# adaLN block on one core: a preparation with every engine in source order, statistics before conditioning, and one group's operands moved first

## The chip, the core and the metric

The kernel runs on one core of a Trainium2 chip. The core has five engines with instruction queues of their own: TensorE (PE, matmuls and transposes, with a weight load that the profile shows as PEld), VectorE (DVE), ScalarE (ACT), GpSimd (POOL) and SyncE (SP). [...] The metric is the device time of one execution in microseconds (us), the median of three runs.

## The reference, cut to what matters

Four sequences (B = 4) of 1024 rows with 256 features go through an attention and a feed-forward layer. A condition vector per sequence gives shift, scale and gate for both.

```python
mod = (_silu(L0_c) @ L0_wmod).reshape(L0_c.shape[0], 6, 1, -1)
sa, ca, ga, sb, cb, gb = (mod[:, 0], mod[:, 1], mod[:, 2], mod[:, 3], mod[:, 4], mod[:, 5])
...
h = _layernorm(x, axis=-1) * (1 + ca) + sa
x = x + ga * _L0_attn_ref(h, L0_attn_xpos, L0_attn_qkv_w, L0_attn_proj_w, L0_attn_proj_b)
h = _layernorm(x, axis=-1) * (1 + cb) + sb
x = x + gb * _L0_ffn_ref(h, L0_ffn_W_base, L0_ffn_b_base, L0_ffn_W_enc, L0_ffn_b_enc, L0_ffn_W_dec, L0_ffn_b_dec, L0_ffn_W_down, L0_ffn_b_down, L0_ffn_W_up, L0_ffn_b_up, L0_ffn_connected_idx)
```

The attention has 16 heads of 16 features and a softmax. The feed-forward layer finds, for each sequence of 256 rows in the reference's view, which of eight small encoders and decoders restores its input best, and adds that one's adapter to a common linear layer. `ga` and `gb` are kept at least 0.25 from zero.

## The kernel before, in words

**The work and its tiles.** A batch is taken as eight tiles of 128 rows, in two halves of 512 (half 0 and half 1). The heads are in four groups of four; a (batch, group) pair is the unit of the attention. For each there is a pass that finds the row maxima of the scores (`ps`, line 448, reduced by DVE into `mx`, line 455), a short way that turns those maxima into a row and stores it as matmul operand (`pmx` L416, `mfull`, POOL's `mrow`, a write to DRAM by L423 and a read-back `mt` by L431), and a pass that computes the scores again with the maximum subtracted by a second matmul (`pt`, L542), takes their exponential on ACT (`es`, L550) and multiplies by v (`pv`, L506). The second pass of a group runs beside the first pass of the next. Queries and keys are each split into two parts of shorter mantissa (`qhl`, `khl`, L348 and L349), and `expand` (L393 to 403) moves them by DMA into the operand tiles `q64`, `k64`: for one group and one pair of heads four transfers of 128 KB for q and four for k, so 16 for a group.

**The preparation**, before the loop over the groups. `load_two` (L84) brings two tiles of x at a time; `qn` is the qkv weight as it lies in memory, `wm` the modulation weight, `pn` the projection's. Then, in source order:

- `condition` (L140 to 151): two transposes of the condition (`pc`), an exponential on ACT, and three small DVE operations that end in `cs`, the sigmoid-weighted condition.
- `turn_weights` (L153): two transposes of one 128-row part of a weight (`pw`) and a copy by ACT. Parts 0 to 3 are q and k, 4 and 5 are v.
- `modulation` (L160): 16 matmuls with `cs` (`pm`, L167) and two DVE copies into `modc`, the shift and scale.
- `norm_first`, a list of work items from `norm_items` (L252): for each half four times `bn_stats` and `bn_aggr` (L260, L261), `ve` (L265), POOL's `rstd` (L267), four centrings (`xh`, L272, on DVE for batch 0 and on POOL for the others), transposes `ptn` (L284) and ACT's `hT` with shift and scale (L285), which needs `modc`.
- `qk_chunk` (L326): the projection of q and k for groups 0 and 1, `expand` for groups 0 and 1, constants, memsets (L921, L937, L942) and `load_rest` (L199 to 215).
- The first sixteen maxima of group 0, with the items of `beside` among them, one after each: the turns of weights 4 and 5, four tiles of v (`pvp`, L370), the second modulation, the gates' rows (`pg`, L182, which POOL shapes and SP writes to DRAM), the turns of the projection weight and the biases.

**What sets the order.** PE's order is the order in the source (`manual_schedule`). In the preparation and in the rest, the order of DVE, ACT, POOL and SP is found by the framework's scheduler, which places instructions by modelled costs; an instruction of a later part can thus go ahead of an earlier one. Each engine works in its order and waits where its next instruction has to wait. In the built program a DMA issue waits until the transfer eight issues earlier has landed.

**The steady stage** (from the loop over `order`, 256 steps, 64 for a batch) is planned in the source: streams of items, of which "X" runs at once, "D" and "R" take a place on PE, "wait" holds a stream for so many steps, "need" until another item is done, "at" and "by" give a step. `defer(n, f)` calls f after n ticks (one tick a step). `turned` (L463) and its `flip`, `back` and `scaled` carry the sums of the softmax through DRAM and multiply by their reciprocal; `post` (L556) is the projection, second norm and feed-forward layer of the batch before; `fixed` (L997) loads, norms and projects the next batch.

Of the kernel before, what the change touches and what calls it, by code (L numbers as in the profile page):

```python
# [17 lines left out]
P = 128  # L18
# [8 lines left out]
def tile_adaln_block(  # L27
# [21 lines left out]
    nc = tc.nc  # L49
    B, S, D = x.shape  # L50
    NE, _, FH = w_enc.shape
    R = w_down.shape[2]
    NT = S // P
    NC = D // P
# [6 lines left out]
    TH = HALF // P  # L61
# [17 lines left out]

    prep = ExitStack()  # L80
    stage = prep.enter_context(tc.tile_pool(name="stage", bufs=1))
    ctx.enter_context(tc.manual_schedule(engines={mybir.EngineType.PE}))

    def load_two(b, u):  # L84
        src = x[b].rearrange("(t p) d -> p t d", p=P)
# [10 lines left out]
    qn = stage.tile([P, 3 * NC, D], F32, name="qn")  # L96
# [1 line left out]
    nc.scalar.dma_start(qn[:, : 2 * NC, :], qkv_rows[:, : 2 * NC, :])  # L98
    wm = stage.tile([P, NC, 6 * D], F32, name="wm")
    wmod_rows = wmod.rearrange("(c p) e -> p c e", p=P)  # L100
    nc.sync.dma_start(wm[:, :, : 2 * D], wmod_rows[:, :, : 2 * D])
    for u in range(NT // 4, NT // 2):
        x_in[0, u] = load_two(0, u)
    nc.scalar.dma_start(qn[:, 2 * NC :, :], qkv_rows[:, 2 * NC :, :])
    nc.scalar.dma_start(wm[:, :, 2 * D :], wmod_rows[:, :, 2 * D :])
    pn = stage.tile([P, NC, D], F32, name="pn")
    nc.scalar.dma_start(pn, proj_w.rearrange("(o p) i -> p o i", p=P))


    ident = cst.tile([P, P], F32, name="ident")  # L110
# [42 lines left out]
    def turn_weights(dst, src, o, tile):  # L153

        pt = tile([P, NC, P], f"pw_{dst.name}_{o}")
        for c in range(NC):
            nc.tensor.transpose(pt[:, c, :], src[:, o, c * P : (c + 1) * P], ident)
        nc.scalar.copy(dst[:, :, o * P : (o + 1) * P], pt)
# [74 lines left out]
    def defer(steps, f):  # L233
        later.append([steps, f])
# [228 lines left out]
    def turned(b, ch, h):  # L463

        n = ch * NH + h
        few = [GC * HG * HALF // P, P]
        rs = st.tile([P, few[0]], F32, tag="rs", name=f"rs_{b}_{ch}_{h}", bufs=2)
        nc.sync.dma_start(rs, sdram[n].rearrange("j (a c) -> (j a) c", c=few[0]))

        def flip():  # L470
            nc.vector.reciprocal(rs, rs)
            nc.sync.dma_start(rdram[n].rearrange("j (a c) -> (j a) c", c=few[0]), rs)

        def back():
            su = wp.tile([P, HALF], F32, tag="su", name=f"su_{b}_{ch}_{h}", bufs=1)
            nc.sync.dma_start(su, rdram[n].unsqueeze(1).to_broadcast([GC * HG, HD, HALF]))
            defer(1, lambda: scaled(b, ch, h, su))

        defer(1, flip)
        defer(2, back)  # L480

    def scaled(b, ch, h, su):
        part = aT_of[b, h][:, ch, :]
        nc.gpsimd.tensor_tensor(part, part, su, ALU.mult)  # L484
# [10 lines left out]
    def step_of(b, g):  # L495

        n = b * NG + g
        va = vaug[n % NV]
        ch, r0 = g // GC, (g % GC) * HG * HD
        acc = {}  # L500

        def weigh(h, kt, es):
            if kt == 0:
                acc[h] = accp.tile([P, HALF], F32, tag="acc", name=f"pv_{b}_{g}_{h}")
            for j in range(HG):
                nc.tensor.matmul(  # L506
                    acc[h][j * STRIP : (j + 1) * STRIP, :],
                    va[:, kt, j, :],
                    es[j // 2][:, j % 2, :],
                    start=(kt == 0),  # L510
                    stop=(kt == NT - 1),
                )
            if kt == NT - 1:
                if (b, h) not in aT_of:
                    aT_of[b, h] = wp.tile([P, NC, HALF], F32, tag="aT", name=f"aT_{b}_{h}", bufs=3)
                ou = wp.tile([P, HALF], F32, tag="ou", name=f"ou_{b}_{g}_{h}", bufs=1)
                nc.scalar.copy(ou, acc[h])
                to = slice(r0, r0 + HG * HD)
                nc.sync.dma_start(aT_of[b, h][to, ch, :], ou[0::2, :])
                if (b, ch) == (B - 1, NC - 1):  # L520
                    if h not in last_su:
                        last_su[h] = wp.tile([P, HALF], F32, tag="su", name=f"su_{b}_{ch}_{h}", bufs=1)
                    nc.sync.dma_start(last_su[h][to, :], ou[1::2, :])
                    if g == NG - 1 and h < NH - 1:
                        defer(2, lambda: scaled_last(h))
                        defer(4, lambda: done.add((b, ch, h)))
                    return
                j0 = (g % GC) * HG
                nc.sync.dma_start(sdram[ch * NH + h][j0 : j0 + HG, :], ou[1::STRIP, :])
                if g % GC == GC - 1:  # L530
                    defer(1, lambda: turned(b, ch, h))
                    defer(8, lambda: done.add((b, ch, h)))

        def begin(h, kt, i, es):

            pt = big_tile([P, 2, HALF], f"pt_{b}_{g}_{h}_{kt}_{i}")
            hs = slice(h * HALF, (h + 1) * HALF)
            q, k = duos["q", b, g, i], duos["k", b, g, i]
            for first in (True, False):
                for a in range(2):  # L540
                    r = slice(a * DUO, (a + 1) * DUO)
                    nc.tensor.matmul(  # L542
                        pt[:, a, :],
                        k[r, kt * P : (kt + 1) * P] if first else picks[i][r, :],
                        q[r, hs] if first else mt[n % 2][r, hs],
                        start=first,
                        stop=not first,
                    )
            e = wp.tile([P, 2, HALF], F32, tag="es", name=f"es_{b}_{g}_{h}_{kt}_{i}", bufs=4)
            nc.scalar.activation(e, pt, AF.Exp, scale=SCALE)  # L550
            es.append(e)

        return begin, weigh


    def post(b, last=False):  # L556
# [231 lines left out]
        def rec(pr, h):  # L788
            return [("R", lambda c=c: decode(pr, c, h)) for c in range(NC)]

        main = [("need", (b - 1, "end")), ("X", load), ("X", alloc), ("wait", 1), ("X", gate_proj)]
        main += [("X", lambda u=u: biased(u, "gpb")) for u in range(NT // 2)]
        for h in range(NH):
            main += [("need", (b, ch, h)) for ch in range(NC)]
# [7 lines left out]
                encs += [("take", "half"), enc(pr, h), ("done", (b, pr, "e", h))]  # L802
                recs += [("need", (b, pr, "e", h))] + rec(pr, h) + [("give", "half")]
        recs.append(("done", (b, "r")))
        tail = [("need", (b, "r")), ("wait", 3), ("D", 0.1, [choose]), ("X", gate_out)]
        tail += [("X", lambda u=u: biased(u, "gbb")) for u in range(NT // 2)]
        tail += [("wait", 1), ("D", FULL, [lambda c=c: narrow(c) for c in range(NC)]), ("wait", 1)]
        each = [(u, t) for u in range(NT // 2) for t in range(2)]
# [69 lines left out]
    def all_of(*streams, most=10**9):  # L878

        took = True  # L880
        while took and most > 0:
            took = False
            for s in streams:
# [5 lines left out]
                if item is not None:  # L889
# [3 lines left out]
                    took, most = True, most - 1  # L893
                    break

    cs = condition()
    for o in range(2 * NC):
        turn_weights(wqkv, qn, o, big_tile)
    modulation(SA, big_tile)
    all_of(Stream(norm_first(0)))  # L900
    all_of(Stream(qk_chunk(0, 0)))
    for g in range(2):
        for i in range(2):
            expand(0, g, i)
    mean_w = cst.tile([P, P], F32, name="mean_w")
    nc.gpsimd.memset(mean_w, 1.0 / (S * D))
    iota_i = cst.tile([P, NE], I32, name="iota_i")
# [48 lines left out]
    nc.gpsimd.tensor_tensor(part_r, part_f, upper, ALU.add)  # L956


    beside = [lambda o=o: turn_weights(wqkv, qn, o, spare_tile) for o in range(2 * NC, 3 * NC)]
    beside += [lambda item=item: [f() for f in item[2]] for item in v_all(0)]  # L960
    beside += [lambda: modulation(SB, spare_tile), lambda: gate_rows(spare_tile)]
    beside += [lambda o=o: turn_weights(wproj, pn, o, spare_tile) for o in range(NC)]
    beside.append(lambda: turn_biases(spare_tile))
# [1 line left out]
    FIRST = PAIRS // NH  # L965
    for n in range(FIRST):
        next(maxima)
        if beside:
            beside.pop(0)()
    tick()  # L970
    all_of(Stream(list(urgent)))
# [2 lines left out]
    tick()  # L974
    given = FIRST + 4
    prep.close()
    wp = ctx.enter_context(tc.tile_pool(name="wp", bufs=2))

    def all_maxima():
# [17 lines left out]
    def fixed(b):  # L997

        moves, work = [], []
        k0 = b * BATCH  # L1000

        def moved(g, i):
            return ("X", lambda: expand(*groups[b * NG + g + 2], i))

        for g in range(NG):
            if b + 1 < B or g < NG - 2:
                key = ("qk", b + (g + 2) // NG, (g + 2) % NG // GC)
                moves += [("at", k0 + g * STEPS + 1), ("need", key), moved(g, 0), moved(g, 1)]
                moves.append(("done", ("moved", b, g)))
        if b + 1 < B:  # L1010

            def load(u):
                x_in[b + 1, u] = load_two(b + 1, u)

            between = [("need", (b - 1, "n", 0))] if b else []
            first = norm_first(b + 1, between + [("X", lambda: load(NT // 2 - 1))])
            if b == 0:
                work += qk_chunk(0, 1) + [("by", 8), ("done", ("qk", 0, 1))]
            work += [("X", lambda u=u: load(u)) for u in range(NT // 2 - 1)] + [("wait", 2)] + first
            work += [("need", ("moved", b, 1)), ("wait", 2)] + qk_chunk(b + 1, 0)  # L1020
            work += [("by", k0 + 2 * STEPS + 8), ("done", ("qk", b + 1, 0))]
            work += [("at", k0 + 3 * STEPS + 1)] + v_all(b + 1)
            work += [("need", ("moved", b, 3)), ("at", k0 + 3 * STEPS + 5)] + qk_chunk(b + 1, 1)
            work += [("by", k0 + 4 * STEPS), ("done", ("qk", b + 1, 1))]
        return [moves, work]
# [180 lines left out]
```

## Time and profile before

| what | value |
|---|---|
| median of three runs | 1190.61 us (1190.61, 1190.59, 1194.73) |
| profiled execution | 1194.91 us |
| its span | 1193.1 us |
| mean granted PE clock | 0.978 of full |
| PE, DVE, ACT, POOL busy | 90%, 66%, 58%, 21% of the span |
| matmuls | 6324 |

The profile comes from one profiled execution, whose time is 4.30 us above the median of the runs; the span is the time from its first to its last record. A page gives the busy time of each engine, then the span in 40 equal slices, in which a digit is the busy share in tenths. Groups of instructions follow with their line, tile names (out<-in), count, busy time and mean. Other views are taken from the same trace: a table of stretches, the timeline of one engine (start, duration, operation, count, and in brackets the idle time before it with what ended it), waits, and the chain of waits, which goes back from the last instruction through what released each step. "issue" is time in which an engine waited for nothing that the profile shows.

### The profile page before, as it was taken

The page shows a single profiled execution, that of the slowest core. Times are in us where ns is not written, and L with a number is a line of the kernel's source. Part 1 is how long each engine was busy: PE and PEld are TensorE (multiplying, and loading weights), DVE is VectorE, ACT ScalarE, POOL GpSimd, SP SyncE. Part 2 cuts the span into 40 slices and gives each one's busy share as a digit, 9 for nine tenths or more (in the row PEclk, how much of TensorE's full clock was granted, in tenths as well). Part 3 has the DMA queues.
Part 4 walks back from the last instruction along what each step waited for, and adds up shares of the span by engine and source line. Part 5 has one row for each costly group of instructions (what it writes and reads, how often), then busy time and mean ns, then how long its engine had stood idle before and what let it go on. Part 6 is the DMA issues. An engine that isn't in the chain of part 4 may idle for free.

```text
span 1193.1 us, 16436 instructions
## 1 busy us (share of the span) xinstructions
PE 1077.8 (90%) x6324; PEld 476.5 (40%) x6324; DVE 791.9 (66%) x975; ACT 692.3 (58%) x928; POOL 254.8 (21%) x271
## 2 busy tenths in 40 slices
PE   4768889999999889999999889999999889899995
PEld 3423333434444333345444333345444333344443
DVE  4477977777687666767678666676778777701264
ACT  2114466665666677654556667654655676647662
POOL 3155000200314002240224201140222200042003
PEclk9869999999999999999999999999999999999998
DMA  6522130122121201113131200204040300011001
GB/s 203 142 81 55 41 77 18 50 69 54 44 60 36 61 15 48 54 43 82 38 110 27 56 15 24 64 27 103 17 131 8 76 1 18 15 58 53 18 1 47
DMA packets 42582, 63.92 MB, mean 54 GB/s; under 512 B 13052, under 2 KB 28436, under 8 KB 42504
## 3 DMA queue, kind: packets, MB, share of 16 engines
q1 hardware_dynamic: 40000, 58.41, 18.2%
q10 hardware_dynamic: 1736, 3.15, 0.8%
q0 software_dynamic: 768, 1.31, 0.5%
q8 instruction: 50, 0.82, 0.3%
q14 instruction: 28, 0.23, 0.1%
HBM read 19.39 MB, written 5.19 MB: 21 GB/s over the span
## 4 chain that ended last, share of the span: by engine, by line
PE 69%; ACT 11%; DVE 10%; DMA 4%; issue 4%; POOL 2%; SPq 0%; ACTq 0%; DVEq 0%; POOLq 0%
PE pt L542 18%; PE pv L506 18%; PE ps L448 10%; ACT es L550 6%; DVE mx L455 5%; PE ph L626 4%; PE pr L647 3%; PE pq L338 3%; PE pvp L370 3%; ACT df L655 3%; DVE df L650 3%; PE ppj L591 2%; PE pf L761 2%; PE pk L338 2%; PE ptn_n L284 2%
## 5 line engine op out<-in xcount | busy, mean ns | idle before, releaser
L455 DVE TENSOR_REDUCE mx<-ps 128x2 f32<-128x1024 f32 x512 | 611.8, 1220 | 191.9 <-PE ps L448 188.2
L550 ACT ACTIVATE es<-pt 128x1024 f32<-128x1024 f32 x512 | 510.8, 1022 | 296.2 <-PE pt L542 289.5
L506 PE MATMUL pv<-es,vaug 128*32 128x512 f32 x2048 | 274.6, 607 | 0.1
L448 PE MATMUL ps<-k,q 64*128 64x512 f32 x1024 | 236.4, 461 | 35.0 <-ACT es L550 10.4
L542 PE MATMUL pt<-q,k 64*128 64x512 f32 x1024 | 239.0, 451 | 21.8 <-ACT es L550 10.7
L542 PE MATMUL pt<-mt,pick 64*128 64x512 f32 x1024 | 209.4, 393 | 4.6 <-DMA mt<-mdram 4.6
L448 PEld LDWEIGHTS ps<-k,q 64*128 64x128 f32 x1024 | 98.3, 186 | 201.4 <-issue 92.5
L542 PEld LDWEIGHTS pt<-q,k 64*128 64x128 f32 x1024 | 99.3, 184 | 170.7 <-DVE mx L455 96.8
L655 ACT ACTIVATE df<-df,fbias 128x512 f32<-128x512 f32 x128 | 91.1, 713 | 55.0 <-DVE df L650 55.0
L542 PEld LDWEIGHTS pt<-mt,pick 64*128 64x128 f32 x1024 | 100.4, 186 | 15.6 <-DMA mt<-mdram 5.8
L650 DVE TENSOR_TENSOR df<-pr,h2T 128x1024 f32<-128x1024 f32 x64 | 77.4, 1222 | 42.5 <-PE pr L647 20.7
L506 PEld LDWEIGHTS pv<-es,vaug 128*32 128x32 f32 x2048 | 40.5, 108 | 100.1 <-issue 90.8
L647 PE MATMUL pr<-he,wdec 64*128 64x512 f32 x256 | 64.3, 614 | 6.3 <-ACT es L550 6.2
L484 POOL TENSOR_TENSOR aT<-aT,su 128x512 f32<-128x512 f32 x14 | 17.8, 1273 | 238.9 <-DMA su<-rdram 189.5
L626 PE MATMUL ph<-h2T,wenc 128*128 128x512 f32 x128 | 63.6, 623 | 0.0
L781 DVE TENSOR_TENSOR x<-pf,x 128x512 f32<-128x512 f32 x16 | 10.8, 687 | 54.3 <-PE pf L772 22.1
L353 POOL CAST qhl<-fu_q 128x512 fp32r<-128x512 f32 x14 | 8.5, 610 | 178.4 <-ACT fu_q L352 175.9
L267 POOL TENSOR_TENSOR rstd_n<-ve_n,neghalf 128x4 f32<-128x4 f32 x16 | 16.8, 1048 | 102.2 <-DVE ve_n L265 96.4
L761 PE MATMUL pf<-wbg,h2T 128*128 128x256 f32 x128 | 37.4, 425 | 0.0
L647 PEld LDWEIGHTS pr<-he,wdec 64*128 64x128 f32 x256 | 21.6, 185 | 37.3 <-ACT es L550 13.2
L284 PE MATMUL ptn_n<-ident,xh_n 128*128 128x128 f32 x128 | 23.2, 311 | 14.0 <-ACT h2T L285 6.6
L626 PEld LDWEIGHTS ph<-h2T,wenc 128*128 128x128 f32 x128 | 22.3, 192 | 33.0 <-issue 31.8
(134 smaller groups left out, 755.8 us busy)
## 6 DMA issues: line engine op xcount, KB each, us to landing
q<-qhl SPq DMA_DIRECT2D x128, 128.0 KB
k<-khl SPq DMA_DIRECT2D x120, 128.0 KB
xin<-in_L_attn_x_dram SPq DMA_DIRECT2D x16, 256.0 KB
x<-in_L_attn_x_dram SPq DMA_DIRECT2D x8, 512.0 KB
aT<-ou SPq DMA_DIRECT2D x32, 128.0 KB
out_dram<-x SPq DMA_DIRECT2D x16, 256.0 KB
su<-rdram SPq DMA_DIRECT2D x14, 256.0 KB
wm<-in_L_wmod_dram ACTq DMA_DIRECT2D x1, 1024.0 KB
```

Source lines behind the costliest of these rows:

```text
L284: nc.tensor.transpose(pt[:, t, :], s["xh"][:, t, c * P : (c + 1) * P], ident)
L338: nc.tensor.matmul(pq, wqkv[:, c, n * D + ch * P : n * D + (ch + 1) * P], hT[:, c, hs], start=(c == 0), stop=(c == NC - 1),)
L448: nc.tensor.matmul(ps[:, a, :], q[r, t0 : t0 + P], k[r, h * HALF : (h + 1) * HALF], start=True, stop=True,)
L455: nc.vector.tensor_reduce(mx[:, h, hq, i::2, t], ps, AX.X, ALU.max, negate=True)
L506: nc.tensor.matmul(acc[h][j * STRIP : (j + 1) * STRIP, :], va[:, kt, j, :], es[j // 2][:, j % 2, :], start=(kt == 0), stop=(kt == NT - 1),)
L542: nc.tensor.matmul(pt[:, a, :], k[r, kt * P : (kt + 1) * P] if first else picks[i][r, :], q[r, hs] if first else mt[n % 2][r, hs], start=f ...
L550: nc.scalar.activation(e, pt, AF.Exp, scale=SCALE)
L626: nc.tensor.matmul(s["ph"], wenc[:, c, 2 * pr : 2 * pr + 2, :].rearrange("p n h -> p (n h)"), s["h2T"][:, c, hs], start=(c == 0), stop=(c ...
L647: nc.tensor.matmul(two[:, i, :], wdec[r, pr, c * P : (c + 1) * P], he[r, :], start=True, stop=True)
L650: nc.vector.tensor_tensor(df, two, h2T[:, c, hs].unsqueeze(1).to_broadcast([P, 2, HALF]), ALU.subtract)
L655: nc.scalar.activation(df[:, i, :], df[:, i, :], AF.Square, bias=bdec_of(e, c), accum_out=s["acc"][:, e, c, h : h + 1],)
L761: nc.tensor.matmul(po[u][:, t, :], s["h2T"][:, c, t0 : t0 + P], s["wbg"][:, c, :], start=(c == 0), stop=False,)
```

## The change

What it does:

- The preparation, up to the point where its pools are closed, also has ACT, DVE, POOL and SP in source order. Loads are given to other queues: the first third of `wm` from SP to ACT, the v part of `qn`, the rest of `wm` and `pn` from ACT to SP, behind the x of half 1.
- Half 0's statistics come before `condition`, half 0's centrings before the weight turns and the modulation, and the rest of the norm after them. `all_of(stream, most=n)` runs n items.
- Only group 0's operands are moved before the constants and `load_rest`; group 1's after the fourth maximum. Weights 4 and 5 are turned right after group 0's `expand`, and two v tiles are computed ahead of the first maximum. The other items of `beside` come after every second maximum.
- In the steady stage, several delays are one or more steps longer.

Lines of the changed kernel are four higher than those of before from the loads on (`ps` L452, `mx` L459, `expand`'s DMA L406).

```diff
+    begin_order = ctx.enter_context(ExitStack())
+    begin_order.enter_context(tc.manual_schedule(engines={ET.Activation, ET.DVE, ET.Pool, ET.SP}))
...
-    nc.sync.dma_start(wm[:, :, : 2 * D], wmod_rows[:, :, : 2 * D])
+    nc.scalar.dma_start(wm[:, :, : 2 * D], wmod_rows[:, :, : 2 * D])
     for u in range(NT // 4, NT // 2):
         x_in[0, u] = load_two(0, u)
-    nc.scalar.dma_start(qn[:, 2 * NC :, :], qkv_rows[:, 2 * NC :, :])
-    nc.scalar.dma_start(wm[:, :, 2 * D :], wmod_rows[:, :, 2 * D :])
+    nc.sync.dma_start(qn[:, 2 * NC :, :], qkv_rows[:, 2 * NC :, :])
+    nc.sync.dma_start(wm[:, :, 2 * D :], wmod_rows[:, :, 2 * D :])
...
-    nc.scalar.dma_start(pn, proj_w.rearrange("(o p) i -> p o i", p=P))
+    nc.sync.dma_start(pn, proj_w.rearrange("(o p) i -> p o i", p=P))
...
-            defer(1, lambda: scaled(b, ch, h, su))
-        defer(1, flip)
-        defer(2, back)
+            defer(2, lambda: scaled(b, ch, h, su))
+        defer(2, flip)
+        defer(3, back)
...
-                    defer(8, lambda: done.add((b, ch, h)))
+                    defer(9, lambda: done.add((b, ch, h)))
...
-        main = [("need", (b - 1, "end")), ("X", load), ("X", alloc), ("wait", 1), ("X", gate_proj)]
+        main = [("need", (b - 1, "end")), ("X", load), ("X", alloc), ("wait", 2), ("X", gate_proj)]
...
-        tail = [("need", (b, "r")), ("wait", 3), ("D", 0.1, [choose]), ("X", gate_out)]
+        tail = [("need", (b, "r")), ("wait", 3), ("D", 0.1, [choose]), ("wait", 1), ("X", gate_out)]
...
+    first_norm = Stream(norm_first(0))
+    all_of(first_norm, most=TH + 2)
     cs = condition()
+    all_of(first_norm, most=TH)
     for o in range(2 * NC):
         turn_weights(wqkv, qn, o, big_tile)
     modulation(SA, big_tile)
-    all_of(Stream(norm_first(0)))
+    all_of(first_norm)
     all_of(Stream(qk_chunk(0, 0)))
-    for g in range(2):
-        for i in range(2):
-            expand(0, g, i)
+    for i in range(2):
+        expand(0, 0, i)
+    for o in range(2 * NC, 3 * NC):
+        turn_weights(wqkv, qn, o, big_tile)
...
-    beside = [lambda o=o: turn_weights(wqkv, qn, o, spare_tile) for o in range(2 * NC, 3 * NC)]
-    beside += [lambda item=item: [f() for f in item[2]] for item in v_all(0)]
+    beside = [lambda item=item: [f() for f in item[2]] for item in v_all(0)]
+    for n in range(2):
+        beside.pop(0)()
...
-        if beside:
+        if n == 4:
+            for i in range(2):
+                expand(0, 1, i)
+        if n % 2 and beside:
             beside.pop(0)()
...
     prep.close()
+    begin_order.close()
...
-            first = norm_first(b + 1, between + [("X", lambda: load(NT // 2 - 1))])
+            first = norm_first(b + 1, between + [("X", lambda: load(NT // 2 - 1)), ("wait", 3)])
...
-            work += [("X", lambda u=u: load(u)) for u in range(NT // 2 - 1)] + [("wait", 2)] + first
+            work += [("X", lambda u=u: load(u)) for u in range(NT // 2 - 1)] + [("wait", 4)] + first
```

## The prediction

> **What bounds the kernel now.** First the page: the busy table and the 40 slices (29.8 us each).
>
> ```profile
> PE 1077.8 (90%) x6324; PEld 476.5 (40%) x6324; DVE 791.9 (66%) x975; ACT 692.3 (58%) x928; POOL 254.8 (21%) x271
> PE   4768889999999889999999889999999889899995
> PEclk9869999999999999999999999999999999999998
> ```
>
> TensorE (PE) is nearly full from the fourth slice on; the first two are half empty and the second and third have a low clock. So a change of the preparation can win only in the first 90 us. The table by stage says how each stage differs.
>
> ```profile
> 0.00:20.00 20.00, 2.65 (x11) 1.69 (x11) 9.83 (x33) 2.95 (x6) 8.61 (x18) 1.00 0.89 272
> 20.00:42.40 22.40, 14.53 (x48) 9.35 (x48) 6.91 (x29) 5.45 (x8) 9.04 (x15) 0.90 0.46 118
> 42.40:62.10 19.70, 19.63 (x76) 11.72 (x76) 10.04 (x10) 3.88 (x18) 0.00 (x0) 0.77 0.43 111
> 62.10:90.00 27.90, 17.44 (x68) 7.67 (x68) 23.62 (x34) 5.58 (x8) 18.30 (x16) 0.68 0.28 87
> 120.00:1100.00 980.00, 919.55 (x5627) 398.68 (x5629) 679.53 (x780) 610.70 (x777) 190.68 (x196) 1.00 0.18 49
> ```
>
> The columns are the stretch, its length, the busy time of PE, its weight load, VectorE (DVE), ScalarE (ACT), GpSimd (POOL), then clock, DMA share and GB/s. Up to 20 us PE works 2.65 us while DMA is at 0.89; from 42.40 to 62.10 PE is the bound; then DVE (23.62 of 27.90). The chain of waits names what holds the front:
>
> ```profile
> 9.74 10.19 issue
> 19.92 3.55 PE pm L167 x16
> ...
> 27.28 3.87 PE pq L338 x8
> ...
> 38.46 4.00 DMA q<-qhl
> ...
> 62.68 9.15 DVE mx L455 x8
> ```
>
> PE waits 10.19 us with nothing shown, then multiplies the modulation (pm). The timeline of DVE tells whom it waited for: pm reads `cs`.
>
> ```profile
> 11.64 0.75 DVE L260 BATCH_NORM_STATS2 bs_n<-xin 128x6 f32<-128x256 f32 x2 [5.79 <-DMA xin<-in_L_attn_x_dram]
> 13.14 0.75 DVE L260 BATCH_NORM_STATS2 bs_n<-xin 128x6 f32<-128x256 f32 x2 [0.53 <-DMA xin<-in_L_attn_x_dram]
> 14.22 3.46 DVE L272 TENSOR_SCALAR xh_n<-xin,mv_n,rstd_n 128x256 f32<-128x256 f32 x6
> 17.59 0.99 DVE L147 TENSOR_SCALAR ex<-ex 128x8 f32<-128x8 f32 x1
> 19.68 0.14 DVE L150 TENSOR_TENSOR cs<-pc,ex 128x8 f32<-128x8 f32 x1
> ```
>
> The sigmoid's three small operations stand behind the statistics of half 1, which wait for x at 11.64 and 13.14, and behind six centrings, so `cs` ends at 19.82. Two more lines, PE and ACT, give the second hold:
>
> ```profile
> 35.22 7.62 ACTq L402 DMA_DIRECT2D k<-khl  x8
> 42.47 0.80 PE L448 MATMUL ps<-k,q 64*128 64x512 f32 x2 [7.91 <-DMA q<-qhl]
> 43.92 0.37 ACT L158 COPY wqkv<-pw_wqkv 128x256 f32<-128x256 f32 x1 [8.73 <-PE pw_wqkv L157]
> ```
>
> The first scores wait until 42.47 for four q and four k transfers; ACT issues eight k transfers until 42.84, one after another.
>
> **The change, part by part.**
>
> *1. Statistics first, sigmoid second, and x ahead of the weights.* Half 0's statistics start at 3.69 and end at 5.84 as now; the sigmoid (0.99, 0.18 and 0.14 us, each beside something else) can end at about 7.1. Four weight turns (2.31 us) follow the first part of qn; that lands for PE at 7.05 now and I take 6.7, as less is in flight ahead of it: 9.0. The first third of wm has landed by 8.29, when the next issue that waits for it goes out in the queue of before; it now goes by ACT's queue behind qn, and I take 9.0. Then 16 pm matmuls: 3.55 us at 19.92, 1.95 us later (56.38); I take 2.55, so 11.6, and modc at 12.0 (0.3).
>
> *2. Half 1.* DVE now does its statistics after modc. With `ve` they took 2.15 us for half 0, and in the built order two statistics of batch 1 stand among them (0.7), so `ve` ends at 15.0. Those two wait for batch 1's first x, now queued on SP behind half 1's x, qn, wm and pn. Through it 3.93 MB must move: at the 272 GB/s of the first 20 us it lands at 14.4, and is asked for at about 14. This is an **added wait** with the whole norm behind it, bounded by nothing and by 5 us (3.93 MB at the first slice's 203 GB/s: 19.4); I take 0.1, as the 272 is measured over these very bytes: 15.1. POOL's rstd takes 1.05 to 1.24: 16.3. Then four centrings: 0.41 us alone, 1.0 us beside POOL's memsets (17.66 and 18.75). The memsets now follow this rstd, so I count two of each, 2.9: 19.2. Transposes of the last quarter 1.1: 20.3. In before these centrings hid behind `cs`.
>
> *3. First projection.* pq and pk: 3.87 us for the first eight now, 1.93 for four later (100.59), 3.53 at a clock of 0.57 (89.33). The first four decide q's first half, the next four its second. I take 3.3 and 1.93: 25.6. Copy and subtraction 0.58 and 0.1 until the first q issue: **26.3 in place of 31.78, a gain of 5.5 us** (4.3 with pm, pq slow; 6.9 with both warm). Without any of it the gain is nil.
>
> [...] PE now idles between the transposes of half 0 (about 14) and those of half 1 (about 18), where before it ran from 19.92 without a break. The row: the granted clock is 1.00 up to 20 us with PE at 2.65 of 20 us, and pm took 3.55 there against 1.95 later. [...]
>
> *4. Group 0's operands first.* Call the first q issue T0. k's first issue comes 3.44 us behind it now, and the fourth k transfer lands 7.1 us after its issue, in a stream that lands one each 0.645 us (11 in 7.1). Moving group 1's sixteen transfers away does not shorten the line for the first eleven. I take 0.3 gained here.
>
> *5. Two v tiles before the first scores.* Here a **new wait** begins. The copies of weights 4 and 5 (2 x 0.37) stand on ACT behind its eight k issues, which end at T0+11.06 now, and pvp needs them. So pvp starts at about T0+11.75, whereas the first scores start at T0+10.69 now. Queued behind pvp on PE are all scores. What follows holds the same PE work less two weight turns (43.20 to 43.81 and 44.54 to 45.16): 19.66 - 1.23 = 18.4; to it I add 0.4, since two pvp tiles now come at the low clock (one took 3.07, the next 1.99). So the ninth scores start at T0+30.55, against 62.13 now, that is T0+30.35: **0.2 lost.** The eight maxima (9.15 us) then go as now. If the k issues end later, each us is a us lost; if the weight copies had come earlier, a us would be gained.
>
> *6. Other loads.* load_rest goes behind eight q issues on SP, group 1's operands behind the fourth maximum. Group 1 is read at about 106 us, and they would be issued by 60. conn's index is used by POOL before the gates (62.90 now) and lands about 46. Cover for all of them is 10 us or more; without it the gates' write and, behind it on SP, the row's write (73.91) would slip. One x load of 256 KB is now between the row's write and its read-back: 0.3 us lost (0 to 0.66, the pace of such loads), since PE waits there 2.20 us for it (78.87). In the next DVE stretch (78 to 88, batch 1's second statistics wait for x at 83.28) rows change places: I take 0.3 lost, within 1 either way.
>
> *7. Delays in the steady stage.* More steps (4.25 us each) between issue and use of sums, gates and norms. They take waits away or postpone work. PE idles 65 us of the stage in pieces below 2 us, none on q or k. The closest cover I found: batch 2's and 3's last k projection stands 95 PE rows ahead of the scores that use it, 149 before (at 3.9 rows a us, 24 us and 38 us); the transfers need about 13, and batch 1 lives with 54 rows. I take 0, between -2 and +2 (the span is 3% idle, and the moved waits are a few of 256 steps).
>
> **The sum.** 5.5 + 0.3 - 0.2 - 0.3 - 0.3 (order) = 5.0 us. The profiled execution took 1194.91 (span 1193.1): it would be 1189.9. It lies 4.3 us above the median 1190.61, on which the forecast stands: **1185.6 us**.
>
> **The rivals.**
>
> *A, a bigger gain (18%).* PE stays warm (pm 1.95, pq 1.93, worth 2.0) and less traffic beside the fetch brings the k issues to an end a us or two early, so pvp starts at once. For: 1.00 clock up to 20 us, DMA share 0.46 in the fetch. Against: 3.55 us for pm. Gain 8: 1182.5, down to 1178 with the steady stage's 2 and the front's best.
>
> *B, little left (14%).* The front comes early and the gain is given back where DVE and x meet at 78 to 88 us, or in the wait for batch 1's x (part 2, up to 5). For: DVE is 23.62 busy of 27.90 there; x landed only at 85.78. Against: that x is asked for earlier when all is earlier. Gain 0 to 3: about 1189.
>
> *C, slower (8%).* The k issues stay behind. load_rest's transfers (now beside k's, where x and weights went before) share the DMA with them, and each issue waits for the landing of one eight issues earlier. One place: ACT's eighth k issue. It ends at T0+11; the gain of 5.0 is gone when it ends after T0+16, and past T0+22 the kernel is over 0.5% slower, about 1197. For: 1.5 MB move beside it, and the same loads held SP 2.66 and 3.55 us at 7.02 and 9.72. Against: the fetch stage moves 118 GB/s where 272 were reached, and 1.5 MB at 272 are 5.5 us, not 11. That the changed orders do nothing at all is in B.
>
> **How the numbers follow.** The main case has 60%; by part 3's bounds and the steady stage's 2 us its own range is 1182.2 to 1188.8. A measurement of this kernel can tell about 0.5%, 5.95 us. The forecast lies just inside that bound: the main case puts 0.24 beyond it and 0.36 within, A all faster, B all within, C slower: faster 0.42, same 0.50, slower 0.08. The range reaches from A's low end, 1178, to B's with 2 us of steady loss and a little of C, 1194.
>
> **What would show it.** In the changed profile: pm at about 9, the idle 10.19 gone; first q issue at about 26; DVE's half-1 statistics not waiting for batch 1's x; ACT's k issues ending at about 37 and pvp at 38, ahead of the first scores; the first eight maxima from about 57; 120 to 1100 with the same PE share. I am wrong if PE's idle time after pm exceeds 6 us, if a k issue ends after 42, or if the steady stage moved over 2 us.

## The result and the profile after

| | median of runs, us | profiled execution | its span | clock |
|---|---|---|---|---|
| before | 1193.0 (five runs, 1190.59 to 1194.73) | 1194.91 | 1193.1 | 0.978 |
| changed | 1203.8 (five runs, 1200.87 to 1205.11) | 1203.8 | 1201.7 | 0.973 |

The changed kernel is **slower**: ratio 1.0089, 95% interval 1.0067 to 1.0111, some 10.6 us. The forecast was 1185.6 us, 5.0 us below the 1190.61 us that were then known of before (the median of three runs).

The page of the changed kernel:

```profile
PE 1086.1 (90%) x6324; PEld 479.6 (40%) x6324; DVE 793.6 (66%) x975; ACT 692.3 (58%) x928; POOL 254.8 (21%) x271
PE   6658899999998889999998889999999889899995
PEclk9879999999998999999999999999999999989998
```

PE does the same 6324 matmuls in 8.3 us more busy time, and the clock row has an 8 in the thirteenth slice (360 to 390 us) and in the thirty-sixth (1051 to 1081 us), where before's had only 9s from the fourth slice to the last but one. The front did what it should. PE's timeline:

```profile
9.06 3.54 PE L171 MATMUL pm<-cs,wm 128*128 128x4 f32 x16 [0.50 <-DVE xh_n L276]
...
21.63 6.01 PE L342 MATMUL pq<-hT,wqkv 128*128 128x512 f32 x8
27.48 3.60 PE L342 MATMUL pk<-hT,wqkv 128*128 128x512 f32 x8
30.91 0.60 PE L161 MATMUL pw_wqkv<-ident,qn 128*128 128x128 f32 x4
40.46 5.15 PE L374 MATMUL pvp<-wqkv,hT 128*128 128x256 f32 x16 [8.95 <-ACT wqkv L162]
45.54 0.73 PE L452 MATMUL ps<-k,q 64*128 64x512 f32 x4
```

The modulation starts at 9.06 (19.92 before), and the v tiles wait 8.95 us for the weight copies, as step 5 said. What became of it shows when one counts the 512 exponentials of the second pass, which stand in the same order in both traces:

| exponential | before, us | changed, us | difference |
|---|---|---|---|
| 16 | 125.1 | 120.1 | -5.0 |
| 144 | 351.0 | 347.0 | -4.0 |
| 272 | 626.1 | 627.9 | +1.8 |
| 400 | 901.8 | 909.0 | +7.2 |
| 511 | 1124.7 | 1133.8 | +9.1 |

Five us are won in the front, and 14 are lost in the steady stage, most between 350 and 900 us. One place on PE there, first in the changed kernel, then in before:

```profile
357.54 0.39 PE L452 MATMUL ps<-k,q 64*128 64x512 f32 x2
357.86 0.66 PE L288 MATMUL ptn_n<-ident,xh_n 128*128 128x128 f32 x4
359.55 0.66 PE L288 MATMUL ptn_n<-ident,xh_n 128*128 128x128 f32 x4 [1.03 <-ACT hT L289]
361.08 3.54 PE L595 MATMUL ppj<-wpg,aT 128*128 128x256 f32 x8 [0.87 <-ACT hT L289]
```

```profile
358.86 0.66 PE L284 MATMUL ptn_n<-ident,xh_n 128*128 128x128 f32 x4
360.39 0.66 PE L284 MATMUL ptn_n<-ident,xh_n 128*128 128x128 f32 x4 [0.87 <-ACT hT L285]
360.97 0.50 PE L448 MATMUL ps<-k,q 64*128 64x512 f32 x2
...
363.98 1.99 PE L591 MATMUL ppj<-wpg,aT 128*128 128x256 f32 x8
```

Both norm transposes and the projection `ppj` use the one spare PSUM tile (`msc`), which ACT must empty (0.78 us) before the next may write it. Before, scores (in the big tiles) follow the second transpose, and `ppj` comes 3 us later. Now `ppj` follows at once: PE stands a second time, and then runs `ppj` in 3.54 us in place of 1.99. The table of stretches of the changed kernel says why (columns as in the prediction):

```profile
355.00:357.40 2.40, 2.40 (x20) 1.06 (x22) 1.52 (x3) 1.07 (x2) 0.30 (x1) 1.00 0.00 0
357.40:360.80 3.40, 1.77 (x14) 0.94 (x10) 2.24 (x2) 2.25 (x3) 0.00 (x0) 1.00 0.00 0
360.80:364.30 3.50, 3.22 (x8) 2.52 (x8) 0.00 (x0) 0.22 (x1) 0.00 (x0) 0.51 0.02 5
364.30:368.00 3.70, 3.70 (x27) 1.68 (x25) 3.23 (x8) 1.94 (x2) 0.28 (x1) 1.00 0.00 0
```

PE is 52% busy in 357.40 to 360.80, and gets half the clock in the next 3.4 us, which costs half of it, 1.7 us. In the order of PE there are four such places (at 357.9, 441.4, 638.8 and 719.1 us) and none before: half 0's transposes with a projection tile, half 1's with an encoder tile (`ph`), in each of two batches. Only the first and the last of the four are followed at once by half clock.

### The profile page after: what moved, and what is told of

It is laid out like the page before. It is cut to its first block, busy times and chain, and to the rows that moved or that the text cites. A ratio compares the mean times of both kernels' runs of the same rounds, so it can differ in the third digit from the quotient of the medians.

```text
span 1201.7 us, 16433 instructions
## 1 busy us (share of the span) xinstructions
PE 1086.1 (90%) x6324; PEld 479.6 (40%) x6324; DVE 793.6 (66%) x975; ACT 692.3 (58%) x928; POOL 254.8 (21%) x271
## 4 chain that ended last, share of the span: by engine, by line
PE 71%; ACT 12%; DVE 10%; issue 3%; DMA 2%; POOL 1%; ACTq 0%; SPq 0%; DVEq 0%; POOLq 0%
PE pv L510 19%; PE pt L546 18%; PE ps L452 10%; ACT es L554 6%; DVE mx L459 4%; PE ph L630 4%; PE pr L651 3%; ACT df L659 3%; DVE df L654 3%; PE pq L342 3%; PE pvp L374 3%; PE ppj L595 3%; PE pk L342 3%; PE pf L765 2%; PE ptn_n L288 1%
## 5 line engine op out<-in xcount | busy, mean ns | idle before, releaser
L459 DVE TENSOR_REDUCE mx<-ps 128x2 f32<-128x1024 f32 x512 | 612.0, 1220 | 203.7 <-PE ps L452 201.6
L452 PE MATMUL ps<-k,q 64*128 64x512 f32 x1024 | 236.4, 462 | 29.6 <-ACT es L554 11.9
L452 PEld LDWEIGHTS ps<-k,q 64*128 64x128 f32 x1024 | 97.9, 186 | 194.6 <-issue 83.4
L374 PE MATMUL pvp<-wqkv,hT 128*128 128x256 f32 x128 | 33.1, 404 | 8.9 <-ACT wqkv L162 8.9
L276 POOL TENSOR_SCALAR xh_n<-xin,mv_n,rstd_n 128x256 f32<-128x256 f32 x24 | 29.0, 1223 | 44.8 <-PE pr L651 44.5
L424 POOL CAST mrow<-mfull 32x128 fp32r<-32x128 f32 x17 | 4.8, 282 | 156.0 <-DVE mfull L422 156.0
L638 ACT ACTIVATE he<-ph,fbias 128x512 f32<-128x512 f32 x32 | 21.8, 682 | 26.4 <-PE ph L630 26.4
```

The lines of the kernel that those rows point to most:

```text
L374: nc.tensor.matmul(pv[:, t, :], hT[:, c, t0 : t0 + P], wqkv[:, c, 2 * D : 3 * D], start=(c == 0), stop=(c == NC - 1),)
L452: nc.tensor.matmul(ps[:, a, :], q[r, t0 : t0 + P], k[r, h * HALF : (h + 1) * HALF], start=True, stop=True,)
L459: nc.vector.tensor_reduce(mx[:, h, hq, i::2, t], ps, AX.X, ALU.max, negate=True)
```

## The experiments

Each was timed in five rounds beside before (median 1193.7 to 1193.8 there). In the expectations theory 1 puts the loss on the longer delays of the steady stage, theory 1a on the norm's two waits and the doubled use of the spare tile.

**Only the front.** All the delays are set back: `scaled`, `flip`, `back`, `done`, the waits in `post` and those in the next batch's norm.

> The changed kernel with all delays of the steady stage as before: only the preparation differs from before (median of before 1193.0 us). Theory 1 (the longer delays in the steady stage cost about 13 us and the front gains 5): 1188 us, ratio 0.996, and none of the four places where a use of the single spare PSUM tile follows two norm transposes on PE. Rival (the delays are harmless, and the loss comes from the new preparation, by the other engines' orders or by the place of stalls against a fixed raster of the clock): about 1204, ratio 1.009.

Measured: 1189.3, ratio 0.9967 (0.9951 to 0.9982). Its exponentials run 4.3 us ahead of before's at number 16 and 4.0 ahead at 496: the steady stage is the same. Theory 1 holds.

**Only the delays**, on before.

> The kernel before with only the longer delays of the steady stage. Theory 1 (the delays are the loss): 1193 + 13 = 1206 us, ratio 1.011, with clock dips behind PE's doubled stalls in batches 1 and 2. Rival (delays harmless, loss from the new preparation): 1193, ratio 1.000.

Measured: 1205.55, ratio 1.0118 (1.0091 to 1.0145). The rival is out.

**Only the norm's waits set back**

```diff
-("X", lambda: load(NT // 2 - 1)), ("wait", 3)])
+("X", lambda: load(NT // 2 - 1))])
-for u in range(NT // 2 - 1)] + [("wait", 4)] + first
+for u in range(NT // 2 - 1)] + [("wait", 2)] + first
```

> The changed kernel with only the two waits in the next batch's norm as before (2 in place of 4, and no 3 between the halves). Theory 1a (these waits move the norm's transposes next to a projection or an encoder tile on PE, both need the one spare tile, PE stands twice and the clock is halved for a while): 1188 to 1192 us, ratio 0.996 to 0.999. Rival (the delays of the sums and gates are the loss): 1204, ratio 1.009.

Measured: 1189.34, ratio 0.9971 (0.9950 to 0.9991): all of the loss is gone.

**Only the sums' delays set back** (`scaled` 2 to 1, `flip` 2 to 1, `back` 3 to 2, `done` 9 to 8).

> The changed kernel with only the delays of the softmax sums (scaled, flip, back, done) as before. Theory 1a (the norm's waits are the loss): 1202 to 1204 us, ratio 1.008. Rival (sums delayed, so projections and all behind them come late): 1189 to 1193, ratio 0.997 to 1.000.

Measured: 1200.64, ratio 1.0068 (1.0044 to 1.0092): the loss stays, within the intervals.

**The waits kept, the neighbours parted**

```diff
-                small, tiles = small - 1, tiles if now is False else 0
+                small, tiles = small - 1, 0
```

> The changed kernel with all its longer delays, and one line of the planner changed: behind a small item (a norm's two transposes) no projection or encoder tile is placed on PE in the same place any more. Theory 1a (not the longer waits cost, but that they put a use of the spare tile right behind two norm transposes, so that PE stands twice): back to 1188 to 1191 us, ratio 0.996 to 0.998. Rival (the waits make the next batch's norm late, or shift the steady stage in other ways): about 1202, ratio 1.008.

Measured: 1189.55, ratio 0.9964 (0.9945 to 0.9984). With all the new delays, the loss goes when no tile follows the transposes. So the waits cost by where they put things on PE. From 340 to 730 us PE's waits (us in total, times, longest) in this run keep the first stall of each place and not the second:

```profile
PE ptn_n L288 <- ACT hT L289: 4.8, 4, 1.4
```

Its trace shows a clock of 1.00 in 400 to 494, 550 to 644 and 700 to 794 us, where the changed kernel's has two spells of half clock, at 722.6 and 784.1. The changed kernel has two more lines of waits:

```profile
PE ptn_n L288 <- ACT hT L289: 4.8, 4, 1.4
...
PE ppj L595 <- ACT hT L289: 1.7, 2, 0.9
PE ph L630 <- ACT hT L289: 1.7, 2, 0.9
```

Before has the first stall alone, and shorter:

```profile
PE ptn_n L284 <- ACT hT L285: 3.7, 4, 1.0
```

**One wait each**, on the front-only kernel: 4 in place of 2, and the 3 between the halves.

> The front-only kernel (ratio 0.9967) plus only the wait 4 in place of 2 ahead of the next batch's norm. It makes two of the four places (half 0's transposes, then a projection tile, in batches 1 and 2's stages). Theory 1a: half the loss, 5 to 7 us over the front-only kernel, 1194 to 1196, ratio 1.001 to 1.003. Rival (the loss goes with the number of steps waited, 2 of 5): 4 to 5 us. Rival (all in the other wait): 1189.

Measured: 1198.51, ratio 1.0040 (1.0021 to 1.0060), 8.7 us over front-only by the ratios: more than theory 1a's 5 to 7, and more than either rival.

> The front-only kernel plus only the wait of 3 steps between the halves of the next batch's norm. It makes the other two of the four places (half 1's transposes, then an encoder tile). Theory 1a: the rest of the loss of the changed kernel over the front-only one (12 us in all, 8.7 of it with the other wait): 3 to 6 us, 1192 to 1195, ratio 0.999 to 1.002. Rival (only the other wait costs): 1189, ratio 0.9967.

Measured: 1194.63, ratio 1.0019 (1.0001 to 1.0037). Each makes its two places, and 0.0073 and 0.0052 over front-only add to 0.0125 where both together make 0.0122 (14.6 us, and not the 12 of the expectation): two places of either kind cost 6 to 9 us.

**What made the front's gain.** The scheduler's order again for ACT, DVE, POOL and SP (the `begin_order` line for them left out):

> The front-only kernel (ratio 0.9967) without the source order of ACT, DVE, POOL and SP: the new source, loads and queues stay, the scheduler orders those engines again, and in the built program the sigmoid stands behind half 1's statistics and most centrings once more. Theory (the order on DVE makes the front's gain): most of the gain is gone, ratio 0.9985 to 1.000, the modulation's matmuls at 13 us or later. Rival (the queues and the smaller first fetch make it): 0.9967.

Measured: 1203.01, ratio 1.0083 (1.0064 to 1.0103), slower than both expectations. `cs` ends at 19.65 again, the first tile of v waits for the copy of weight 5 behind the k issues (to 43.73), the row of maxima is written at 75.09 (73.91 before), and exponential 48 is 7.0 us late. Half of that comes where rival B placed a loss: DVE waits 5.62 us, until 93.07, for batch 1's x, which stands ahead of three maxima in its order (1.80 us, until 85.80, in before). So the order carries the gain, and without it the new source loses.

> The front-only kernel with the loads of the weights on their old queues (the first third of wm on SP ahead of half 1's x; the rest of wm and qn and pn on ACT). Theory (order, not queues): half 1's x lands at 11 to 13 us, about when DVE asks for it at 12.8, so 0 to 1 us lost, ratio 0.9967 to 0.9975. Rival (the queues make the gain): 0.999 to 1.000.

Measured: 1188.41, ratio 0.9959 (0.9945 to 0.9973): the queues give nothing that can be told.

> The front-only kernel with the whole norm behind the conditioning and the modulation in source order, so also on DVE. Theory (the interleaving counts as much as the source order): half 0's statistics, rstd and centrings, 5 us, move behind the modulation at 12.7 us into the path, ratio 1.000 to 1.001. Rival (PE and the loads hide them): 0.9967.

Measured: 1192.69, ratio 1.0009 (0.9991 to 1.0028): the interleaving is worth the 5 us, and the source order without it gains nothing that can be told.

**More from the front.** Copies of weights 4 and 5 ahead of the k issues:

```diff
+    for o in range(2 * NC, 3 * NC):
+        turn_weights(wqkv, qn, o, big_tile)
     for i in range(2):
         expand(0, 0, i)
-    for o in range(2 * NC, 3 * NC):
-        turn_weights(wqkv, qn, o, big_tile)
```

> The front-only kernel (ratio 0.9967) with the turns and copies of weights 4 and 5 ahead of the k transfers' issues on ACT, not behind. Theory (the v tiles and, behind them on PE, all scores wait 8.95 us for copies that stand behind eight k issues): the v tiles run in that idle time, first scores at about 40 in place of 45.5, 4 to 5 us gained: 1184 to 1185, ratio 0.993. Rival (the scores wait for the k transfers anyway, or the gain is lost to the later wait for the maxima's way through DRAM): 1188 to 1190, ratio 0.996 to 0.997.

Measured: 1184.86, ratio 0.9918 (0.9900 to 0.9935). PE's timeline:

```profile
31.70 3.72 PE L374 MATMUL pvp<-wqkv,hT 128*128 128x256 f32 x16 [0.79 <-ACT wqkv L162]
38.56 0.85 PE L452 MATMUL ps<-k,q 64*128 64x512 f32 x4 [3.13 <-DMA k<-khl]
```

The v tiles are done before the operands land, which are waited for now.

And POOL's memsets behind half 1's last centring:

```diff
+            if name == "n1_0_1" and t == TH - 1:
+                late = cst.tile([P, 1], F32, name="late")
+                nc.gpsimd.tensor_copy(late, s["xh"][:, t, 0:1])
```

> The kernel of the run before this one, and POOL's memsets made to wait for half 1's last centring by a copy of one column. Theory (centrings take 3.52 us beside the memsets and 1.38 alone, and the whole front hangs on them): 2 us more gained, 1182 to 1183, ratio 0.991; centrings 1.4 us. Rival (PE gets no faster for it, or the later memsets hold something up): no further gain, ratio 0.993 or above.

Measured: 1181.27, ratio 0.9893 (0.9872 to 0.9914), **the best version**, 1.1% faster than before. Its interval overlaps that of the run above; in the traces its exponential 16 comes 3.0 us earlier (112.0, 115.0). DVE's centrings in the changed kernel and here:

```profile
16.71 3.52 DVE L276 TENSOR_SCALAR xh_n<-xin,mv_n,rstd_n 128x256 f32<-128x256 f32 x4 [0.67 <-POOL rstd_n L271]
```

```profile
16.90 1.38 DVE L276 TENSOR_SCALAR xh_n<-xin,mv_n,rstd_n 128x256 f32<-128x256 f32 x4 [0.67 <-POOL rstd_n L271]
...
19.32 6.11 DVE L269 TENSOR_SCALAR ve_n<-mv_n 128x4 f32<-128x4 f32 x1
...
22.93 2.50 DVE L356 TENSOR_TENSOR qhl<-pq,qhl 128x512 fp32r<-128x512 f32 x1
```

Now DVE stands elsewhere: a 128x4 operation of batch 1's statistics (`ve`), 0.77 us long in the changed kernel, takes 6.11 and ends at 25.43, and the subtraction that starts behind it ends there too, 2.50 us long where 0.69 was seen. PE waits for that, so some of the 2.1 us came back:

```profile
25.55 3.70 PE L345 MATMUL pk<-hT,wqkv 128*128 128x512 f32 x8 [1.56 <-DVE qhl L356]
```

## Why the prediction was wrong

**Step 7 failed**: "I take 0, between -2 and +2". The same edits alone cost 12 us by the medians and 14 by the ratio (1.0118), and the prediction's own sign of being wrong, a steady stage moved over 2 us, came true. The step looked for a transfer or wait that the new distances would bring, and for cover ahead of the scores; the waits moved no transfer into the path. They moved an item in PE's order next to another that needs the same PSUM tile. PE's order is written in the source; a list of its neighbours that share the spare tile shows four rows of three in the changed kernel's steady stage, where before has only pairs.

Of the 18.2 us between 1185.6 and the measured 1203.8, 2.4 are before's own median (1190.61, then 1193.0); 14.5 are the delays (from the ratios 1.0089 and 0.9967), and 1.1 are what the front fell short.

Where the loss is, from one trace each of front-only and changed, between the same exponentials (999.8 and 1013.7 us from number 16 to 511):

| from, to | length, front-only and changed | PE idle | lost to half clock |
|---|---|---|---|
| 16, 144 | 225.9, 226.9 | 12.1, 12.1 | 0, 0 |
| 144, 272 | 275.7, 280.9 | 15.4, 17.5 | 0, 3.4 |
| 272, 400 | 275.6, 281.1 | 15.4, 17.4 | 0, 3.4 |
| 400, 511 | 222.6, 224.8 | 18.2, 18.2 | 1.7, 5.1 |

So 2 us in each of the two middle stretches are the second stalls themselves (0.87 each, with a longer first one), and 3.4 are two spells of half clock. In each of them only one spell comes right behind a place (360.8 and 722.6 us); the others (381.3 and 784.1) follow waits of PE for row maxima. The 2.2 us of the last stretch go with half clock too, at 1040.1 and 1064.0 us, where no such place stands, and the first stretch has 1.0 us more PE work. "PE idles 65 us of the stage in pieces below 2 us" was read as slack; what counted was that two pieces came close together. The reason beside it, "the span is 3% idle", does not fit the prediction's own row, where PE idles 60.45 of 980 us, 6%. That neighbours are the cause of the loss is shown (the run that parts them, and the two runs with one wait each); how it divides between stalls and clock is read from single traces, and that the spells are set off by PE's low share just before was not tried by itself.

**The front, steps 1 to 6, was right in sum**: 5.0 us forecast, 3.9 measured (ratio 0.9967) and 4.3 to 5.0 in the traces. Part of that is luck, for its terms were off both ways: 2.0 us too little ahead of the first q issue, 1.5 too much behind it. The first q issue came at 28.29, not 26.3: pm took 3.54 (2.55 taken), the four centrings 3.52 (2.9), the eight pq matmuls 6.01 (5.23). The row's 1.00 up to 20 us did not mean fast matmuls there: the 16 pm took 3.54 us under it and 1.95 at 51.38 (the last section has the lines). Step 2's added wait for batch 1's x did not come (it landed at 13.9, DVE took it at 14.4). Step 5's new wait came as said, 8.95 us, but the stage behind it was shorter, 16.9 us to the ninth scores at 57.37 and not 18.8: the clock was 0.89 in 42.40 to 62.10 (0.77 before), and two pairs of scores side by side take 0.73, not 2 x 0.50. Step 6: the wait for the read-back rose from 2.20 to 3.05, 0.8 lost where 0.3 was taken.

Rival C, the slower one, was the wrong place: ACT's eighth k issue ended at 39.72, 11.4 us after the first q issue. Rival A's second half was real and open: the front-only kernel lost another 4.9 per mil behind the k issues (0.9967 to 0.9918).

## What to carry to other kernels

A wait given to one stream of a hand-planned order moves its items against all the others: compare the built orders for neighbours that share a buffer with one copy, before pricing the wait itself. Price a stall on PE with the clock that follows it (0.51 in 360.80 to 364.30 us here, 1.7 us lost behind stalls of 1.03 and 0.87), and test a change of several independent parts in parts: here 4 us of gain stood beside 14 us of loss. Where an engine issues DMAs that hold it up, put the small copies that another engine waits for ahead of them (PE's wait of 8.95 us for two copies became 0.79 here).

## What the runs showed of the hardware

Between 340 and 900 us of the changed kernel's trace half clock comes in spells of one length on a fixed raster, that is, whole multiples of one length apart. Its clock records put them at 360.8, 381.3, 722.6 and 784.1 us, each 3.413 us long: 20.5, 361.8 and 423.3 us after the first, which is 6, 106 and 124 times 3.413. The same pair of stalls at 441 to 446 us was cut by the raster (at 442.7) and brought no spell, with PE 55% busy in 442.70 to 446.20; nor did the pair at 639 to 642 us, whose two stretches of the raster have PE 70% and 74% busy:

```profile
442.70:446.20 3.50, 1.92 (x7) 1.09 (x8) 0.00 (x0) 1.43 (x2) 0.00 (x0) 1.00 0.00 0
...
719.20:722.60 3.40, 1.24 (x8) 0.76 (x8) 1.23 (x1) 2.65 (x4) 0.00 (x0) 1.00 0.00 0
722.60:726.00 3.40, 3.30 (x4) 1.17 (x4) 0.00 (x0) 0.05 (x1) 0.00 (x0) 0.51 0.00 0
```

From 100 to 900 us the stretches of the raster ahead of the four spells have PE 52%, 64%, 36% and 58% busy, and others with 55%, 57%, 58%, 63% and 64% were not followed by one, so busy time alone does not tell. Before has no half clock from 92.5 to 1058.4 us, with stretches of 57% and 58% among them (495.30 to 498.70 and 700.10 to 703.50). In 400 to 494, 550 to 644 and 700 to 794 us the other traces with doubled stalls show 2 spells (only the delays), 2 (the sums' delays set back), 3 (the 3 between the halves alone) and none (the 4 alone); of those without, front-only and the parted one show none there, and the one with the norm's waits set back shows one, at 609.6. Of the changed kernel's four only two come right behind a doubled stall; what brings the other two stays open.

In the opening the row shows 1.00 while the 16 pm matmuls take 3.54 us there and 1.95 at 51.38. The trace's first clock record begins at 26.32 us (27.63 in before), and up to there the row reads 1.00. The pq matmuls are slow up to that time, 1.06 us each from 22.65 to 26.06, and the last two, from 26.62 on, take 0.59; two at 23.50, and the last one:

```profile
23.50 1.91 PE L342 MATMUL pq<-hT,wqkv 128*128 128x512 f32 x2
...
27.05 0.59 PE L342 MATMUL pq<-hT,wqkv 128*128 128x512 f32 x1
```
